# A four-layer graph network on one core: finer buffer waits around two attentions, split first transposes, and a diffusion that runs one tile further ahead

## The chip, the core and the metric

The kernel runs on one core of a Trainium2 chip. The core has five engines that each work through their own queue of instructions in order: TensorE (PE in the profile; its weight loads are listed apart as PEld), VectorE (DVE), ScalarE (ACT), GpSimd (POOL), and SyncE (SP), which here only issues DMA transfers. Engines meet through semaphores. The metric is device time in microseconds (us); three runs of the kernel before took 3431.24 (median), 3437.7 and 3429.77.

## The reference

There are 3327 nodes with 256 features, so 26 row tiles of 128 nodes (3328 rows, one of them padding). Four layers follow one another; each adds its result to x and normalizes:

```python
x = _layernorm(x + _L0_gnn_ref(x, adj, W))        # neighbourhood mean
x = _layernorm(x + _L1_gnn_ref(x, adj, ...))      # graph convolution, then a scan over the nodes
x = _layernorm(x + _L2_gnn_ref(x, adj, ...))      # graph attention
x = _layernorm(x + _L3_gnn_ref(x, adj, ...))      # the layer that changes here
```

Only layer 3 matters here. In its two steps a diffusion and an attention run side by side:

```python
for n in range(2):
    A = _top_p_attention(Xa, W1, W2, W3)   # softmax(q k^T), keep the largest that hold 90%, renormalize
    Xf = R @ Xf                            # R = (adj + I), rows divided by their sums
    Xa = A @ Xa
    Z = Z + Xf @ U1[n].T + Xa @ U2[n].T
h = X + Z                                  # then normalized, scaled and shifted
```

## The kernel before

All data are float32. X holds the input of layer 3 in on-chip memory, tile by tile. F (also named Y) receives the diffused rows, G the attended rows. The program shows each float32 matrix product as two records on PE.

**Who sets the order.** The program is traced in Python and then scheduled at build time: an instruction that is ready earlier may be queued ahead of one traced before it, unless it is pinned. `here(...)`, `in_order(...)` and `keep_in_program_order` pin an instruction behind everything traced before on its engine. In the first attention (`fixed = True`) every PE and DVE instruction made through `tensor` and `vector` is pinned. In the second attention the products of the scores (line 1154), the ScalarE copies and the ScalarE passes of the search are pinned; the products of the diffusion (`aggregated`, line 1296) and of the attention (line 1341), most DVE and POOL work and all DMA issues are not. A queue, once made, runs strictly in order.

**Pools.** Buffers come from pools (`tile_pool`). A pool that opens where an earlier one has closed takes over its memory. Without an option, the first user of such memory waits for the whole earlier pool to be finished with.

**First attention** (lines 1656 to 1770; pools l3p, l3a, and l3w, l3s, which live on through the second). A score row of 128 x 3328 is made in four chunks: PE multiplies, ScalarE copies (lines 1160, 1163). Only one score buffer exists in PSUM, so a chunk waits for the copy of the chunk before it. `search_short` then finds the cut on DVE, with a ScalarE exponential (line 1404) in its middle. Tile 0 is diffused in layer 2 (`spread_first`) and tile 1 by `diffused_first`: four adjacency loads (line 1217), 26 products, a `yield` after every fourth. All others run in pairs of tiles. `diffused_pair` does 13 steps of seven half-size products; `attended_pair` does the same with weights that must first be transposed on PE (`turn`), copied by ScalarE (`wt`, line 1263) and combined on DVE (`mix`). Loop `for i in range(nh - 1)` weaves them: `stage` runs seven diffusion steps; at step 5 `attend_to` flushes the pending search and issues the first three `turn`s, twelve transposes in a row, and two `mix`es. `first` then finishes each tile: two projections, keys and queries of the second attention, stores to DRAM (lines 1569, 1579, 909), and ends with `store_keys` (copies at lines 905 and 907). `unresolved` closes the phase with one small product (line 1627).

**Second attention** (lines 1778 to 1841; pools l3q in PSUM, l3at for the adjacency tiles, l3b for the rest). Loop `for i in range(-2, nt + 1)`; a pass of it is called step i here. Step i makes the scores of tile i+2, goes on with `search_long` of tiles i, i+1 and i+2 (ScalarE lines 1436, 1441, 1456, 1458, 1474, 1487; DVE lines 1503, 1353, 1364, 1366, 1532, 1540), attends tile i-1, and diffuses the tiles named by `more`: before, tile i+1, from step -1 on. `slot` hands out three to five diffusion products between two chunks. A diffusion of one tile (`aggregated`) loads six adjacency pieces through three buffers (line 1294), does 26 products and ends in `xf` (DVE line 1315); `xf` has DL + 3 = 4 buffers. `second` finishes tile i-1 (DVE line 1586, POOL, the output store at line 1608). The scores' buffer is single again, three PSUM buffers serve diffusions and attentions, three the transposes.

Of the kernel before, what the change touches and what calls it, by code (L numbers as in the profile page):

```python
# [9 lines left out]
F32 = mybir.dt.float32  # L10
# [5 lines left out]
PSUM = bass.MemoryType.PSUM  # L16
DRAM = bass.MemoryType.DRAM

P = 128
D = 256  # L20
# [22 lines left out]
DL = 1  # L43
# [7 lines left out]
def gnn_kernel(ctx: ExitStack, tc: tile.TileContext, n: int, a: dict, out: bass.AP):  # L51
    nc = tc.nc
    nt = -(-n // P)
# [814 lines left out]
    with tc.tile_pool(name="l3", bufs=1) as pool, tc.tile_pool(name="l3d", bufs=1, space=DRAM) as dram:  # L868
# [383 lines left out]
        def attended_pair(quads, psum, es, b):  # L1252

            pa = psum.tile([P, 2, 512], F32, name="acc")
            wts, ws = [], []

            def turn(j):
                pt = psum.tile([P, 4, P], F32, name="tp")
                for r, e in enumerate(es):
                    for h in range(2):  # L1260
                        tensor.transpose(pt[:, 2 * r + h, :], e[:, (h * nh + j) * P:(h * nh + j + 1) * P], ident)
                wts.append(quads.tile([P, 4, P], F32, name="wt", bufs=4))
                nc.scalar.copy(wts[-1], pt)  # L1263

            def mix():
                wt = wts.pop(0)
                sw = quads.tile([P, 4, P], F32, name="sw", bufs=3)
                vector.tensor_tensor(sw[:, :2, :], wt[:, ::3, :], wt[:, 2:3, :].to_broadcast([P, 2, P]), op=ALU.add)
                vector.tensor_add(sw[:, 2, :], sw[:, 1, :], wt[:, 0, :])
                vector.tensor_add(sw[:, 3, :], sw[:, 2, :], wt[:, 1, :])  # L1270
                a11, a12, a21, a22, s3, s1, s2, s4 = (x[:, k, :] for x in (wt, sw) for k in range(4))
                ws.append((a11, a12, s1, a22, s2, s3, s4))

            for j in range(3):
                turn(j)
            for j in range(2):
                mix()
            yield None
            for j in range(nh):
                if j + 3 < nh:  # L1280
                    turn(j + 3)
                if wts:
                    mix()
                products(pa, j, ws.pop(0), b)
                yield None
            yield assembled(quads, pa)
# [15 lines left out]
        def diffused(work, atp, psum, p, it, out, each=J3):  # L1302

            rd = rdeg[:, it:it + 1]
            t = work.tile([P, D], F32, name="t")
            nc.gpsimd.tensor_scalar(t, (Y if p else X)[:, it, :], rd, None, op0=ALU.mult)
            if p:
                s = work.tile([P, D], F32, name="s")
                nc.sync.dma_start(s, sd[it])
                nc.gpsimd.tensor_tensor(t, t, s, op=ALU.add)  # L1310
            for acc in aggregated(atp, psum, it, Y if p else X, each):
                if acc is None:
                    yield
            d = work.tile([P, D], F32, name="xf", bufs=DL + 3)
            nc.vector.scalar_tensor_tensor(d, acc, rd, t, op0=ALU.mult, op1=ALU.add)
            out.append(d)

# [318 lines left out]
            while parts:  # L1636
                parts = [x for x in parts if next(x, parts) is not parts]

        with tc.tile_pool(name="l3w", bufs=2) as work, tc.tile_pool(name="l3s", bufs=4) as sm:


            def start(p, t, es, searches, search):
# [7 lines left out]
                                     **({"halves": True} if p and t == nt - 1 else {}))  # L1650
                return scores(work, psum, p, q, es[t])

            with tc.tile_pool(name="l3p", bufs=2, space=PSUM) as psum, tc.tile_pool(name="l3a", bufs=1) as quads:
                fixed = True
                es, searches, xfs, todo, queue = {}, {}, [xf0], [], []
                flat = G.rearrange("p t d -> p (t d)")
# [22 lines left out]
                def stage(spread, steps, groups, ends, counts, then):  # L1679
                    for k in range(steps):  # L1680
                        next(spread, None)
                        then.get(k, int)()
                        if k % 2 == 0:
                            next(groups, None)
                        if k in (2, 3, 4):
                            next(ends[0], None)
                        looks(counts[k])
                    for _ in groups:
                        pass
                    for _ in ends[0]:  # L1690
                        pass

                def attend_to(i):
                    turned[0] = attended_pair(quads, psum, (es[2 * i], es[2 * i + 1]), b)
                    finish()
                    next(turned[0])

                turned = [None]
# [11 lines left out]

                groups = logits(0)
                x = diffused_first(quads, psum, 1, xfs)
                for _ in groups:
                    next(x)
                queue.append(searches[0])
# [8 lines left out]
                counts = 7 * [4]  # L1724
                ends = [iter(())]
                for i in range(nh - 1):
                    stage(spread, 7, logits(2 * i + 2), ends, counts,
                          {0: lambda: end_pair(i - 1) if i else None, 5: lambda: attend_to(i)})
                    counts = [1, 2, 2, 2, 2, 0, 0]
                    queue.append(searches[2 * i + 2])  # L1730
                    values = turned[0]
                    for k in range(7):
                        next(values)
                        looks(k in (1, 2, 4, 5, 6))
                    stage(spread, 6, logits(2 * i + 3), todo[1], [2, 1, 2, 1, 2, 1], {})
                    finish()
                    queue.append(searches[2 * i + 3])
                    for k in range(6):
                        next(values)
                        if k == 0:  # L1740
                            for _ in spread:
                                pass
                        if k == 3:
                            spread = spreading(i + 2)
                        looks(k > 1)
# [29 lines left out]

            with tc.tile_pool(name="l3q", bufs=3, space=PSUM) as psum, tc.tile_pool(name="l3at", bufs=3) as atp, \
                    tc.tile_pool(name="l3b", bufs=2) as lone:
                es, searches, xfs = {}, {}, []  # L1780
                result = iter(())
                for i in range(-2, nt + 1):
                    def search(t):
                        if 0 <= t < nt:
                            next(searches[t])

                    values, logits, spread = iter(()), iter(()), iter(())
                    if 0 < i:
                        values = attended(lone, psum, es[i - 1], G, 3, in_order(nc.scalar.copy))
                    if i + 2 < nt:  # L1790
                        logits = start(1, i + 2, es, searches, search_long)
                    more = range(len(xfs), min(nt, i + DL + 1))
                    spread = (x for j in more for x in diffused(lone, atp, psum, 1, j, xfs, 1))

                    def slot(products, looks, pair=False):


                        if pair:
                            next(logits, None)
                        for _ in range(products * len(more)):  # L1800
                            next(spread, None)
                        if pair:
                            next(logits, None)
                        next(values, None)
                        search(looks)

                    search(i)
                    slot(3, i + 1, True)
                    next(result, None)
                    search(i)  # L1810
                    search(i + 1)
                    search(i)
                    next(logits, None)
                    next(result, None)
                    for _ in range(3 * len(more)):
                        next(spread, None)
                    next(logits, None)
                    search(i + 2)
                    next(values, None)
                    search(i)  # L1820
                    next(result, None)
                    slot(3, i + 1, True)
                    slot(3, i + 1, True)
                    for _ in result:
                        pass
                    both(logits)
                    search(i)
                    slot(5, i + 2)
                    search(i + 1)
                    search(i)  # L1830
                    slot(5, i + 1)
                    slot(4, i + 1)
                    both(spread)
                    search(i)
                    if 0 < i:
                        f = normalizer(sm, kepts[1][:, i - 1:i], tots[1][:, i - 1:i])
                        result = second(lone, psum, i - 1, next(values), f, xfs[i - 1])
                both(result)
                edge[0] = None
                fl = unresolved(sm, psum, 1)  # L1840
# [142 lines left out]
```

## Time and profile before

The profiled execution took 3433.03 us itself; its span on the core is 3431.1 us. Its granted TensorE clock is 0.964 on average.

| engine | busy us | share of span |
|---|---|---|
| PE | 3140.4 | 92% |
| PEld | 2565.8 | 75% |
| DVE | 2686.5 | 78% |
| ACT | 1735.4 | 51% |
| POOL | 1127.6 | 33% |

DMA moved 344.31 MB, a mean of 100 GB/s.

A wait is listed as "engine line <- what released it": total us, number of times, longest. A timeline row gives the start, the length, engine, line, operation, output <- input and count, and in brackets the idle time of the engine before it with what ended it. A row of engine PE with x52 holds 26 products. Line 891 is the helper through which all pinned PE and DVE instructions pass, so there the tile's name tells what it is. Layer 3 begins at about 1699.7 us; in the table of stages that the prediction shows, the stages are the opening of the first attention, its steady part, its end, the opening of the second attention, that attention's next five steps, its steady part, its last step with a diffusion, and the rest.

### The profile page before, as it was taken

The page shows a single profiled execution, that of the slowest core. Times are in us where ns is not written, and L with a number is a line of the kernel's source. Part 1 is how long each engine was busy: PE and PEld are TensorE (multiplying, and loading weights), DVE is VectorE, ACT ScalarE, POOL GpSimd, SP SyncE. Part 2 cuts the span into 40 slices and gives each one's busy share as a digit, 9 for nine tenths or more (in the row PEclk, how much of TensorE's full clock was granted, in tenths as well). Part 3 has the DMA queues.
Part 4 walks back from the last instruction along what each step waited for, and adds up shares of the span by engine and source line. Part 5 has one row for each costly group of instructions (what it writes and reads, how often), then busy time and mean ns, then how long its engine had stood idle before and what let it go on. Part 6 is the DMA issues. An engine that isn't in the chain of part 4 may idle for free. (4 is left out here: it accounts for less than half of the span.)

```text
span 3431.1 us, 50276 instructions
## 1 busy us (share of the span) xinstructions
PE 3140.4 (92%) x18301; PEld 2565.8 (75%) x18301; DVE 2686.5 (78%) x5895; ACT 1735.4 (51%) x2764; POOL 1127.6 (33%) x1332
## 2 busy tenths in 40 slices
PE   8999888898988776999989999999998999999996
PEld 5999657676675554888778888888885677777775
DVE  4655368999999997877578778778755898988886
ACT  1000456767767675111133333333337788888883
POOL 0000245666665654111400000000003566656563
PEclk9999999999999988999999999999998999999998
DMA  6775334334343322444322232232213122222220
GB/s 200 251 253 188 105 101 125 110 108 116 102 115 89 69 57 81 150 137 151 115 76 87 65 88 79 69 89 80 71 50 102 52 68 68 64 66 65 72 64 16
DMA packets 206264, 344.31 MB, mean 100 GB/s; under 512 B 22223, under 2 KB 129167, under 8 KB 205871
## 3 DMA queue, kind: packets, MB, share of 16 engines
q1 hardware_dynamic: 205998, 340.92, 33.2%
q8 instruction: 148, 2.42, 0.3%
q14 instruction: 118, 0.96, 0.1%
HBM read 304.65 MB, written 36.21 MB: 99 GB/s over the span
## 5 line engine op out<-in xcount | busy, mean ns | idle before, releaser
L330 POOL TENSOR_TENSOR h<-du,row 128x2048 f32<-128x2048 f32 (+1 forms) x110 | 465.5, 4232 | 344.9 <-DVE hc L330 248.6
L330 DVE TENSOR_TENSOR_SCAN h<-dA,carry,h 128x512 f32<-128x512 f32 (+1 forms) x384 | 449.0, 1220 | 18.2 <-ACT dA L337 18.1
L337 ACT ACTIVATE dA<-t,A_log 128x512 f32<-128x512 f32 (+1 forms) x448 | 292.5, 658 | 147.1 <-DVE h L330 145.5
L1296 PE MATMUL acc<-F,at 128*128 128x256 f32 x1352 | 354.3, 388 | 1.8 <-DMA at<-in_adjT 1.8
L1341 PE MATMUL acc<-G,wt 128*128 128x256 f32 x1352 | 336.6, 392 | 9.7 <-ACT wt L1139 9.3
L1341 PEld LDWEIGHTS acc<-G,wt 128*128 128x128 f32 x1352 | 250.1, 193 | 72.4 <-ACT wt L1139 42.2
L1079 PE MATMUL acc<-F,at 128*128 128x257 f32 x1352 | 303.4, 381 | 0.7 <-ACT r L1023 0.7
L389 PE MATMUL cb<-F,at 128*128 128x256 f32 x1196 | 295.5, 395 | 8.0 <-ACT hn L409 3.4
L1296 PEld LDWEIGHTS acc<-F,at 128*128 128x128 f32 x1352 | 239.3, 191 | 74.9 <-issue 46.6
L1146 POOL MEMSET e<- 128x1 f32 x52 | 4.9, 99 | 838.5 <-PE tp L891 769.5
L1079 PEld LDWEIGHTS acc<-F,at 128*128 128x128 f32 x1352 | 253.3, 190 | 36.2 <-issue 1.0
L680 PE MATMUL y<-ident,hc 128*128 128x128 f32 x1664 | 236.4, 296 | 46.2 <-DVE hc L330 46.1
L680 PEld LDWEIGHTS y<-ident,hc 128*128 128x128 f32 x1664 | 210.4, 154 | 87.4 <-DVE hc L330 62.6
L389 PEld LDWEIGHTS cb<-F,at 128*128 128x128 f32 x1196 | 229.8, 198 | 58.3 <-issue 19.4
L330 DVE TENSOR_TENSOR hc<-h,row 128x2048 f32<-128x2048 f32 (+2 forms) x114 | 243.2, 2135 | 11.3 <-PE y L680 4.3
L891 PE MATMUL acc<-X,at 128*128 128x128 f32 (+1 forms) x988 | 173.7, 287 | 6.0 <-issue 6.0
L1263 ACT COPY wt<-tp 128x512 f32<-128x512 f32 x156 | 90.8, 589 | 166.6 <-PE tp L891 153.2
L138 PE MATMUL acc<-t,cb 128*128 128x128 f32 (+1 forms) x1014 | 168.4, 275 | 0.0
L891 PEld LDWEIGHTS acc<-X,at 128*128 128x128 f32 x988 | 142.2, 193 | 29.9 <-issue 26.1
L891 PE MATMUL acc<-G,sw 128*128 128x128 f32 x936 | 155.5, 275 | 0.0
L891 DVE MAX8 cand<-e 128x8 f32<-128x128 f32 x676 | 139.8, 277 | 5.0 <-ACT e L1160 3.2
L1160 ACT COPY e<-sc 128x832 f32<-128x832 f32 x78 | 65.9, 845 | 149.2 <-PE sc L891 149.1
(414 smaller groups left out, 7263.0 us busy)
## 6 DMA issues: line engine op xcount, KB each, us to landing
at<-in_adjT SPq DMA_DIRECT2D x54, 832.0 KB, 4.5
at<-in_adjT SPq DMA_DIRECT2D x130, 320.0 KB, 3.0
row<-bc SPq DMA_DIRECT2D x80, 512.0 KB, 5.1
at<-in_adjT SPq DMA_DIRECT2D x52, 640.0 KB, 5.5
at<-in_adjT SPq DMA_DIRECT2D x52, 576.0 KB, 4.1
at<-in_adjT SPq DMA_DIRECT2D x72, 256.0 KB, 3.1
at<-mixed SPq DMA_DIRECT2D x72, 256.0 KB, 3.6
mixed<-cb SPq DMA_DIRECT2D x26, 640.0 KB, 4.2
```

The costliest lines, as they stand in the source:

```text
L138: mm = nc.tensor.matmul(acc, w[:, j, :], x, start=(y == 0 and k % 3 == 0 and k < 6), stop=(y == nh - 1 and k in (2, 6)))
L330: return lambda *x, **k: tc.keep_in_program_order(op(*x, **k))
L337: decays.append(op(*x, **k))
L389: ten.matmul(acc, at[:, j % JC, :], X0[:, j, :], start=(j == 0), stop=(j == nt - 1))
L680: x = ten.matmul(y[:, g * P:(g + 1) * P], h[:, g, i * P:(i + 1) * P], ident, is_transpose=True, start=(first and g == 0), stop=(last and g ...
L891: return lambda *x, **k: tc.keep_in_program_order(op(*x, **k))
L1079: nc.tensor.matmul(acc, at[:, j, :], F[:, j0 + j, :], start=(j0 + j == 0), stop=(j0 + j == nt - 1))
L1146: nc.gpsimd.memset(e[:, n:], NEG)
L1160: copy(halves[:, :, c0:c0 + ws[0]], pl[:, :, :ws[0]])
L1263: nc.scalar.copy(wts[-1], pt)
L1296: nc.tensor.matmul(acc, at[:, j, :], rhs[:, j0 + j, :], start=(j0 + j == 0), stop=(j0 + j == nt - 1))
L1341: tensor.matmul(acc, wt[:, j, :], rhs[:, j0 + j, :], start=(j0 + j == 0), stop=(j0 + j == nt - 1))
```

## The change

Five edits, all in layer 3.

1. The pools l3w, l3s, l3p, l3a, l3q, l3at and l3b get `reuse_waits="tile"`: a buffer waits for the last use of its own memory, not for the end of the pool that had it.
2. `attended_pair` yields after each of its first three `turn`s. `attend_to` issues the first; a new function `go_on` issues the second in the last step of `stage`, and the third after `stage`. The two `mix`es follow the second and the third.
3. `stage` counts the calls in `then` from its end.
4. Two chunks of the first score row are made before the loop that alternates chunks with `diffused_first`.
5. In the second attention `more` names tile i+2, one tile per step, from step -2 on; the last step with a diffusion is 23, not 24. `xf` gets a fifth buffer.

```diff
-            for j in range(3):
-                turn(j)
-            for j in range(2):
-                mix()
+            turn(0)
+            yield None
+            turn(1)
+            mix()
+            yield None
+            turn(2)
+            mix()
             yield None
...
-            d = work.tile([P, D], F32, name="xf", bufs=DL + 3)
+            d = work.tile([P, D], F32, name="xf", bufs=DL + 4)
...
-        with tc.tile_pool(name="l3w", bufs=2) as work, tc.tile_pool(name="l3s", bufs=4) as sm:
+        with tc.tile_pool(name="l3w", bufs=2, reuse_waits="tile") as work, tc.tile_pool(name="l3s", bufs=4, reuse_waits="tile") as sm:
...
-            with tc.tile_pool(name="l3p", bufs=2, space=PSUM) as psum, tc.tile_pool(name="l3a", bufs=1) as quads:
+            with tc.tile_pool(name="l3p", bufs=2, space=PSUM, reuse_waits="tile") as psum, tc.tile_pool(name="l3a", bufs=1, reuse_waits="tile") as quads:
...
-                        then.get(k, int)()
+                        then.get(k - steps, int)()
...
+                def go_on():
+                    next(turned[0])
...
                 x = diffused_first(quads, psum, 1, xfs)
+                next(groups)
+                next(groups)
                 for _ in groups:
                     next(x)
...
-                    stage(spread, 7, logits(2 * i + 2), ends, counts,
-                          {0: lambda: end_pair(i - 1) if i else None, 5: lambda: attend_to(i)})
+                    stage(spread, len(counts), logits(2 * i + 2), ends, counts,
+                          {-7: lambda: end_pair(i - 1) if i else None, -2: lambda: attend_to(i), -1: go_on})
+                    go_on()
...
-            with tc.tile_pool(name="l3q", bufs=3, space=PSUM) as psum, tc.tile_pool(name="l3at", bufs=3) as atp, \
-                    tc.tile_pool(name="l3b", bufs=2) as lone:
+            with tc.tile_pool(name="l3q", bufs=3, space=PSUM, reuse_waits="tile") as psum, tc.tile_pool(name="l3at", bufs=3, reuse_waits="tile") as atp, \
+                    tc.tile_pool(name="l3b", bufs=2, reuse_waits="tile") as lone:
...
-                    more = range(len(xfs), min(nt, i + DL + 1))
+                    more = range(len(xfs), min(nt, i + DL + 2, len(xfs) + 1))
```

## The prediction

> **What bounds the kernel now.** I read the table of stages first, then what PE waited for, then the timelines round each seam of layer 3. In the table each row gives a stretch, its length, the busy time of PE, PEld, DVE, ACT and POOL with their instructions, the granted PE clock, the DMA share and GB/s.
>
> ```profile
> 1699.70:1755.50 55.80, 35.67 (x184) 24.05 (x184) 39.67 (x114) 17.43 (x20) 20.18 (x20) 0.89 0.37 111
> 1755.50:2518.00 762.50, 748.20 (x5805) 666.88 (x5806) 608.92 (x2061) 281.73 (x452) 3.28 (x25) 1.00 0.26 75
> 2518.00:2568.80 50.80, 47.22 (x259) 40.77 (x257) 19.21 (x67) 17.29 (x37) 0.20 (x2) 1.00 0.18 56
> 2568.80:2639.20 70.40, 54.40 (x208) 35.09 (x208) 27.66 (x80) 51.07 (x42) 27.54 (x60) 0.84 0.41 128
> 2639.20:2792.00 152.80, 143.01 (x679) 108.73 (x680) 133.59 (x399) 123.73 (x122) 83.65 (x169) 0.97 0.19 54
> 2792.00:3340.00 548.00, 544.36 (x2617) 405.41 (x2616) 489.85 (x1457) 463.29 (x448) 339.08 (x666) 1.00 0.23 66
> 3340.00:3373.30 33.30, 28.11 (x140) 22.99 (x139) 27.39 (x83) 23.55 (x23) 15.71 (x38) 0.97 0.16 46
> 3373.30:3431.10 57.80, 35.19 (x158) 29.27 (x158) 31.44 (x106) 8.87 (x17) 16.72 (x28) 0.80 0.03 9
> ```
>
> Both long stages are bound by PE: 748.20 of 762.50 us and 544.36 of 548.00 us, at full clock; a step of the second lasts 30.6 us. The seams are not: in the two openings PE stands idle for 20 and 16 us and runs at a lower clock. So the change can win only at seams, and from the 14.3 us missing in the first steady stage, which the list of PE's waits there explains whole:
>
> ```profile
> PE tp L891 <- DVE e L891: 11.7, 11, 1.1
> PE tp L891 <- ACT wt L1263: 2.6, 11, 0.2
> ```
>
> Three rows of the first opening: DVE waits for the end of `diffused_first`, and PE then for the masked score row of tile 1.
>
> ```profile
> 1728.95 0.48 DVE L891 SCALAR_TENSOR_TENSOR F<-acc,rdeg,F 128x256 f32<-128x256 f32 x1 [5.79 <-PE acc L891]
> 1753.69 0.45 PE L891 MATMUL tp<-ident,e 128*128 128x128 f32 x1 [8.89 <-DVE e L891]
> 1755.47 2.27 PE L891 MATMUL tp<-ident,e 128*128 128x128 f32 x9 [1.33 <-DVE e L891]
> ```
>
> The second opening: the first scores wait for the last reader of the old pool; the adjacency is requested late; six products (x12) take 5.14 us, 0.857 us each, where three in the steady part take 1.30, 0.433 each; the first transposes wait 9 us for the search.
>
> ```profile
> 2568.78 1.67 PE L1154 MATMUL sc<-kT,q 64*128 64x416 f32 x4 [1.93 <-ACT q L907]
> 2571.73 1.51 SPq L1294 DMA_DIRECT2D at<-in_adjT  x3
> 2581.31 5.14 PE L1296 MATMUL acc<-F,at 128*128 128x256 f32 x12
> 2639.22 1.97 PE L1327 MATMUL tp<-ident,e 128*128 128x128 f32 x8 [9.00 <-DVE e L1540]
> ```
>
> And step 24, where ScalarE's pass waits behind a copy that waits for PE, and DVE at the end of that chain:
>
> ```profile
> 3350.90 0.58 ACT L1139 COPY wt<-tp 128x512 f32<-128x512 f32 x1 [2.58 <-PE tp L1327]
> 3362.70 0.16 DVE L1490 RECIPROCAL s<-s 128x1 f32<-128x1 f32 x1 [2.79 <-POOL s L1444]
> ```
>
> **What the Trainium skill says.** "TensorE: Matmul & The Clock Gate", section "What's actually happening": PE runs at half clock after some 3.4 us of idling and at full clock after as long of work. The trace agrees: 0.857 against 0.433 us per product. The table at the head of that page calls the ScalarE and VectorE queues strict FIFO; so one late operand holds all behind it, as the 2.58 and 2.79 us show. "DMA: Bandwidth & Descriptors", section "Anatomy of one DMA", puts some 2 us of fixed cost on a transfer, for the software path; here a 320 KB adjacency piece lands 3.0 us after its issue.
>
> **The change, part by part.**
>
> *Two score chunks first* (edit 4). Before, chunk 0 of tile 0 is at 1700.44, chunk 1 only at 1711.13, behind four products that wait for adjacency until 1707.4; chunk 3 at 1717.27. Now chunks 0 to 2 go ahead while that load travels: by 0.97 to 1.46 us of product and 0.85 of copy each, from 1702.88 (first copy, after the table load), they are copied at about 1708; four products at the low clock (3.75) and chunk 3 follow, so the row is copied at 1713.2 against 1719.2. No instruction is added. `spreading(1)` comes two products-of-four earlier, so its three DMAs pass the second adjacency load on SP's queue; that load lands near 1711.5, before PE wants it at 1714. PE then has 22 products (9.5 us), four chunks (3.6) less what is done, and at most 3.2 us behind the exponential: `diffused_first` ends near 1726 instead of 1728.9. On DVE ten looks of the search now precede the wait for it, six before; the four rounds (0.87 each, 3.5 us) fill that wait. From that wait's end to e of tile 1 was 1755.5 - 1728.95 = 26.55; it becomes 23.0. So e is ready at 1749.3: -6.2 us. Bounds: DVE's whole 12.2 us of waiting up to there cannot be beaten; with an end at 1729, 3.5. I take -6.2 and keep -3.5 to -8. Its POOL memset of the padding, at 1718.81 behind 23 row scalings, may cost 1.5, inside these.
>
> *Transposes apart* (edits 2, 3). Same instructions. The 1.06 us wait for e stays: `turn(0)` is still in step 5, and its fourth transpose needs the same DVE result. The 0.24 us wait for the first copy goes, since seven products (1.57 us) stand between: 11 x 0.24 = -2.6. A `cb` subtraction on DVE (0.69) may come ahead of a `mix`; PE has the second and third turn and a chunk (1.9) to cover it; uncovered it costs 0.69 x 12 = 8. Bounds -2.6 to 0, or -14.3 if the e wait vanished too, for which I see no cause.
>
> *Waits by buffer, and the extra diffusion at the seam* (edits 1, 5). Scores can start when line 1627 leaves PE, 2566.9; their copies must still follow `store_keys`, 2568.73. First copy 2568.75 against 2570.53. The adjacency issues move from 2571.7 to before 2550, past the stores of `first` on SP's queue (0.33 to 1.1 us each; SP is idle for most of that time), so products of tile 0 fill the gaps between chunks and keep PE at full clock. A chunk then takes 2.25 us (0.9 + 3 x 0.433) instead of 2.7: the last copy ends 2576.0, not 2579.6. Now the price: 14 products of tile 0 (6.1 us) stand ahead of tile 1's first chunk, pinned behind them. It starts near 2582 (before: 2579.62), so the exponential of line 1441 gains only 0.6; at line 1456, where ScalarE waited 2.84 us for cold products, it is 3.0 ahead, and from there the chain to the transposes is the same 47 us: e at 2636.2, -3.0. Bounds: -6 (no delay behind the products) to +2; beyond that see the rivals.
>
> *Where that work goes.* Before, the opening did three diffusions, one more than its steps name, and steps 1 to 9 issued 420 records of line 1296 instead of 9 x 52 = 468: 24 products, 10.4 us, had been done ahead. With tile i+2 due in step i and three diffusions in the opening, nothing is ahead, and these steps hold 10.4 us more PE work. Their PE waits (0.42, 1.63, 0.37, 2.66, 2.37, 2.32, 0.30) sum to 10.1 us and can take it. I take +2; bounds 0 (hidden) to +10.4. The steady steps keep their content: 30.6 each, 0.
>
> *Step 24 without a diffusion.* Transposes reach ScalarE early; the 2.79 us wait goes and `xf` (0.48) leaves DVE's chain, which then bounds to the end: -3.3 (0 to -4).
>
> Sum: -6.2 - 2.6 - 3.0 + 2.0 - 3.3 = -13.1. The profiled execution took 3433.0 (2 beyond its span, which stays), so 3419.9; the median shown is 1.8 lower: **3418**. Own range 3410 to 3425.
>
> **Rivals.** 0.3% of 3431, 10.3 us, is about what a measurement can tell from no change.
> (a) *The work comes back:* the extra 10.4 us do not fit the waits, since these end with DVE's result at a fixed place in the queue. Sum -4.7 (with +10.4): 3427. For it: PE is the bound in all following steps.
> (b) *The old tail takes it:* with adjacency early, unpinned products slip into PE's gaps (3.6 us from 2518 to 2568) and a fourth diffusion into the 9.0 us before the transposes. 26 x 0.433 = 11.3 more: -24, 3407. Against: before, nothing filled those 9 us.
> (c) *Slower:* adjacency still comes at 2574.8, cold. Three products stand before each pinned chunk, and 26 x 0.857 = 22.3 plus three chunks (5.2) put tile 1's first chunk at 2602, 22.7 late; ScalarE's search stands behind its copy. -6.2 - 2.6 + 22.7 - 3.3 = +10.6: 3442. It decides when that chunk starts after 2602.
> (d) *Pool waits stay in effect* but PE is warm: the chunks wait for 2574.8, +5 in place of -3: -5.1, 3426.
>
> **Chances.** Forecast 0.50, (a) 0.19, (b) 0.14, (c) 0.11, (d) 0.06. Below 3421 lie 0.37 of the forecast's 0.50 and (b): faster 0.51. The rest of the forecast, (a) and (d): same 0.37. (c), with disturbances of the same sign: slower 0.12. Range 3403 to 3435: leaves out (c) and the far edge of (b).
>
> **What the profile will show.** Chunk 3 of tile 0 before 1712.5 and the first masked row near 1749 (else the first step fails); no wait for wt L1263 among PE's waits, 11 to 12 us for e left; adjacency issues before 2560 and PE clock over 0.92 in the opening; its first transposes 66 to 68 us after the first score instead of 70.4; steps of 30.6 after; no 2.79 us DVE wait in step 24. Steps longer than 30.6, or another order on PE in them, would break the forecast: 0.5 us there is 11 us.

## The result: slower by 0.5%

The changed kernel takes 3448.03 us, the kernel before 3430.51 us (medians of six runs each on one chip): the ratio is 1.005, with a 95% interval of 1.0037 to 1.0064, so 12.7 to 22 us more. The forecast was 3418, its range ended at 3435. The profiled span grew from 3431.1 to 3446.6 us.

The table of stages of the changed kernel, with the same columns and cut at the same events as before (first score of layer 3, first attention at work, its last products, first score of the second attention, its first transposes; step 24, the last with a diffusion before, without one now):

```profile
1703.56:1764.00 60.44, 42.60 (x184) 27.95 (x185) 39.60 (x114) 17.43 (x20) 20.20 (x20) 0.78 0.33 103
1764.00:2521.10 757.10, 745.44 (x5805) 666.38 (x5806) 611.88 (x2061) 281.76 (x452) 3.31 (x25) 1.00 0.26 75
2521.10:2569.84 48.74, 47.09 (x256) 40.71 (x255) 18.77 (x64) 16.40 (x34) 1.12 (x3) 1.00 0.17 56
2569.84:2654.79 84.95, 63.87 (x262) 43.99 (x261) 28.30 (x83) 51.97 (x45) 23.36 (x60) 0.88 0.43 129
...
3355.50:3390.00 34.50, 19.08 (x85) 15.70 (x85) 27.70 (x88) 22.01 (x21) 14.47 (x36) 0.84 0.01 5
```

Two stages got shorter: the twelve pairs (757.10 after 762.50) and the end of the first attention (48.74 after 50.80). Three got longer: the first opening (60.44 after 55.80, its clock 0.78 after 0.89), above all the second opening (84.95 after 70.40), and step 24. The steps between them kept their length: from the end of step 0's search to that of step 23 it is 699.6 us, 701.2 before.

**The pairs.** In the list of PE's waits in that stage one row is left; the one for wt L1263 is gone:

```profile
PE tp L891 <- DVE e L891: 13.0, 12, 1.3
```

**The first opening.** The timeline (start, length, engine and line, and in brackets the idle time with what ended it), where before DVE had waited 5.79 us and its row stood at 1728.95:

```profile
1722.69 0.18 POOL L1146 MEMSET e<- 128x1 f32 x4
...
1723.82 3.07 ACT L1407 ACTIVATE e<-e,neg 128x3328 f32<-128x3328 f32 x1 [5.70 <-POOL F L1203]
...
1726.89 0.83 ACT L1160 COPY e<-sc 128x832 f32<-128x832 f32 x1
...
1727.78 1.76 PE L891 MATMUL sc<-kT,q 64*128 64x416 f32 x4 [4.14 <-ACT e L1160]
...
1738.29 0.48 DVE L891 SCALAR_TENSOR_TENSOR F<-acc,rdeg,F 128x256 f32<-128x256 f32 x1 [10.70 <-PE acc L891]
```

The same place before:

```profile
1722.93 3.07 ACT L1404 ACTIVATE e<-e,neg 128x3328 f32<-128x3328 f32 x1 [3.73 <-DVE neg L891]
...
1725.99 0.83 ACT L1160 COPY e<-sc 128x832 f32<-128x832 f32 x1
...
1726.88 0.97 PE L891 MATMUL sc<-kT,q 64*128 64x416 f32 x4 [2.17 <-ACT e L1160]
1727.78 1.13 PE L891 MATMUL acc<-X,at 128*128 128x256 f32 x4
```

Three chunks did go first. Then POOL's memset of the padding, behind its row scalings, holds the end of the first looks and so the exponential: it comes 18.4 us after the first score product, 18.3 before, so it did not move with the chunks. The exponential stands on ScalarE ahead of the copy of tile 1's first chunk, as before, but PE now waits 4.14 us for that copy instead of 2.17. And ten of the 26 products of `diffused_first` are still to come behind that wait, where two were left before, because four products stand between two chunks and two chunks have gone ahead. `diffused_first` ends 34.0 us after the first score product, 28.5 before.

**The second opening**, in the same view:

```profile
2569.84 0.97 PE L1154 MATMUL sc<-kT,q 64*128 64x416 f32 x4
...
2573.07 0.46 SPq L1782 DMA_DIRECT2D G<-gd  x1
...
2574.47 1.58 SPq L1297 DMA_DIRECT2D at<-in_adjT  x3
...
2581.81 2.93 PE L1299 MATMUL acc<-F,at 128*128 128x256 f32 x6 [11.01 <-DMA at<-in_adjT]
...
2584.67 1.76 PE L1154 MATMUL sc<-kT,q 64*128 64x416 f32 x4
...
2599.00 0.97 PE L1154 MATMUL sc<-kT,q 64*128 64x416 f32 x4
...
2654.79 2.39 PE L1330 MATMUL tp<-ident,e 128*128 128x128 f32 x10 [7.93 <-DVE e L1543]
```

The first score starts right behind the last product of the first attention. But the adjacency load is issued 4.6 us after it, and three diffusion products that need it stand ahead of the second chunk: PE waits 11.01 us. Of these, 3.7 us pass until the issue at 2574.47, and 7.3 us from there until the first piece lands at 2581.8. In the steps that follow, such a piece lands after a median of 3.0 us; here the pieces travel right behind the reload of G (1664 KB, issued at 2573.07). Tile 1's first chunk comes 29.16 us after the first score (10.84 before), the transposes 84.95 after (70.44).

**Step 24**, which has no diffusion now (34.2 us from the end of the search in step 23 to that in step 24, 32.7 before):

```profile
3372.82 0.60 ACT L1609 ACTIVATE h<-h,nb,rs 128x256 f32<-128x256 f32 x1 [3.50 <-POOL nb L1608]
...
3375.39 0.16 DVE L1493 RECIPROCAL s<-s 128x1 f32<-128x1 f32 x1 [4.21 <-POOL s L1447]
...
3375.47 0.36 DVE L1367 MAX8 top<-rest 128x8 f32<-128x208 f32 x1
```

The 2.79 us wait did not go: it is 4.21 us, and it now stands in the middle of the ranking of tile 24, with four of its six rounds behind it, where before only the last round was behind it.

The sum over the two profiles: opening (first score to second exponential) +4.55, pairs -5.3, from the last exponential to the first score of the second attention -2.0, second opening +14.5, steps 1 to 23 -1.6, step 24 +1.5: +11.7. The remaining 3.8 us of the span's 15.5 lie ahead of the first score product of layer 3, up to which PE's order is unchanged. In the fourteen profiles of this study that product stands anywhere from 1693.5 to 1704.3 us, so this part is read as variation between runs, which no run here tests; spans of single profiles are therefore not compared below, only stages, and times only as ratios.

### The profile page after: what moved, and what is told of

Same layout as the page of the kernel before. It is cut to its first block, busy times and chain, and to the rows that moved or that the text cites. A ratio compares the mean times of both kernels' runs of the same rounds, so it can differ in the third digit from the quotient of the medians.

```text
span 3446.6 us, 50261 instructions
## 1 busy us (share of the span) xinstructions
PE 3142.4 (91%) x18301; PEld 2569.4 (75%) x18301; DVE 2687.3 (78%) x5895; ACT 1735.6 (50%) x2764; POOL 1129.0 (33%) x1332
## 5 line engine op out<-in xcount | busy, mean ns | idle before, releaser
L330 DVE TENSOR_TENSOR_SCAN h<-dA,carry,h 128x512 f32<-128x512 f32 (+1 forms) x384 | 449.0, 1221 | 18.3 <-ACT dA L337 18.1
L1263 ACT COPY wt<-tp 128x512 f32<-128x512 f32 x156 | 90.7, 591 | 181.4 <-PE tp L891 168.6
L1139 ACT COPY e<-sc 128x832 f32<-128x832 f32 (+2 forms) x130 | 90.0, 713 | 106.9 <-PE sc L1154 105.9
```

The source lines that it names most:

```text
L330: return lambda *x, **k: tc.keep_in_program_order(op(*x, **k))
L1139: return lambda *x, **k: tc.keep_in_program_order(op(*x, **k))
```

## The experiments

Each run was timed against the kernel before on the same chip. "Opening" is the time from the first score product of layer 3 to the second exponential, "pairs" from there to the last exponential of the first attention, "gap" from there to the first score of the second attention, "tile 1" from that score to the first chunk of tile 1, "seam" to the first transposes; step 24 from the start of the pass that writes the masked row e in step 23 to that in step 24. All in us, from the profiles.

| kernel | ratio to before (95%) | opening | pairs | gap | tile 1 | seam | step 24 |
|---|---|---|---|---|---|---|---|
| before | 1 | 45.2 | 777.4 | 45.7 | 10.8 | 70.4 | 32.7 |
| changed | 1.0050 (1.0037 to 1.0064) | 49.8 | 772.1 | 43.7 | 29.2 | 85.0 | 34.2 |
| e1 transposes alone | 0.9991 (0.9983 to 0.9999) | 46.6 | 772.6 | 45.7 | 9.9 | 69.4 | 32.8 |
| e2 two chunks alone | 1.0014 (1.0007 to 1.0021) | 49.6 | 776.8 | 45.7 | 8.2 | 67.1 | 32.7 |
| e3 changed, no edit 5 | 1.0001 (0.9993 to 1.0009) | 51.1 | 771.8 | 43.7 | 10.3 | 68.4 | 32.8 |
| e4 changed, load on POOL | 1.0017 (1.0009 to 1.0026) | 50.7 | 771.8 | 43.7 | 23.5 | 77.5 | 34.2 |
| e5 two chunks, exponential later | 0.9994 (0.9984 to 1.0004) | 41.5 | 778.1 | 45.7 | 10.2 | 70.4 | 32.8 |
| e6 changed, products behind row 0 | 1.0027 (1.0017 to 1.0037) | 50.2 | 771.8 | 43.7 | 25.8 | 83.5 | 34.2 |
| e7 edits 1 to 3, load on POOL | 0.9996 (0.9987 to 1.0005) | 45.9 | 772.1 | 43.7 | 18.1 | 72.6 | 32.8 |
| e8 as e7, with e5 | 0.9984 (0.9977 to 0.9992) | 42.5 | 772.3 | 43.7 | 18.3 | 72.7 | 32.7 |
| e9 edit 5 alone | 1.0031 (1.0019 to 1.0043) | 45.2 | 777.2 | 45.7 | 26.5 | 80.4 | 34.2 |
| e10 pools alone | 1.0007 (0.9997 to 1.0016) | 46.3 | 778.0 | 43.7 | 10.8 | 70.2 | 32.8 |
| e11 changed, step 24 reordered | 1.0041 (1.0026 to 1.0057) | 49.1 | 773.0 | 43.7 | 28.1 | 82.5 | 31.2 |
| e12 edits 1 to 3, e5, e11 | 0.9975 (0.9964 to 0.9986) | 44.1 | 772.2 | 43.7 | 8.9 | 70.2 | 32.3 |

A stage at which two kernels have the same order on the queues still differs between profiles: the seam of before and of e2 is 70.4 and 67.1 us. Differences of 3 us at the seam or 1.5 in the opening are not read as effects. Two stretches are not in the table: steps 1 to 23, which take 698.3 to 702.4 us, and what follows step 24, which takes 61.7 us before and 61.8 in the changed kernel, but 62.9 to 63.4 in e2, e3, e7, e8 and e12; why was not followed.

**e1, the transposes alone.** Edits 2 and 3 of the diff, on the kernel before:

```diff
-            for j in range(3):
-                turn(j)
-            for j in range(2):
-                mix()
-            yield None
+            turn(0)
+            yield None
+            turn(1)
+            mix()
+            yield None
+            turn(2)
+            mix()
+            yield None
```

> Edits 2 and 3 alone on the kernel before. Account of the result read from the two traces: the twelve pairs lose 0.4 us each, so -4.8 us, ratio 0.9986, and the list of PE's waits has no row for wt L1263. Rival: the pairs' gain comes from the tile-wise pools (edit 1) and not from the order of the transposes; then 0 us and the row stays. The prediction's term was -2.6.

The pairs lose 4.8 us, the row for wt L1263 is gone from PE's waits, and the ratio of 0.9991 stands for -3.1 us (-0.3 to -5.8). The gain is the transposes', not the pools': e10 has pairs of 778.0.

**e2, two chunks first, alone.** Edit 4:

```diff
                 x = diffused_first(quads, psum, 1, xfs)
+                next(groups)
+                next(groups)
```

> Edit 4 alone on the kernel before. Account: the two chunks ahead are what costs the first opening its 4.5 us (the exponential of tile 0 stands ahead of tile 1's first copy on ACT, and PE waits behind it), so +4.5 us, ratio 1.0013, second exponential about 50 us after the first score product instead of 45. Rival: the loss comes from edit 1, and edit 4 gives what was predicted, -6.2 us, ratio 0.998.

+4.8 us by the ratio (2.4 to 7.2), and 4.4 in the opening, with the same chain as in the changed kernel:

```profile
1718.13 3.07 ACT L1404 ACTIVATE e<-e,neg 128x3328 f32<-128x3328 f32 x1 [6.69 <-POOL F L1203]
...
1722.08 1.76 PE L891 MATMUL sc<-kT,q 64*128 64x416 f32 x4 [5.14 <-ACT e L1160]
...
1723.77 3.39 PE L891 MATMUL acc<-X,at 128*128 128x256 f32 x8
```

Tile 1's first chunk was multiplied at 1714.05 and copied only at 1721.20, behind the exponential; after the 5.14 us wait four products take 3.39 us, where four took 1.99 ahead of it.

**e5, the same with the exponential later.** On e2, the score copies of tiles 0 and 1 and the first exponential are pinned in the program's order:

```diff
-            copy = in_order(nc.scalar.copy) if p else nc.scalar.copy
+            copy = in_order(nc.scalar.copy) if p or pin else nc.scalar.copy
...
-                return scores(work, psum, p, q, es[t])
+                return scores(work, psum, p, q, es[t], t < 2)
...
-                    nc.scalar.activation(e, e, AF.Exp, bias=neg, accum_out=total)
+                    x = nc.scalar.activation(e, e, AF.Exp, bias=neg, accum_out=total)
+                    if early:
+                        early.pop()
+                        here(x)
```

> Edit 4 alone, with the ScalarE copies of tiles 0 and 1 and the first exponential pinned in the order of the program, which puts the exponential behind tile 1's third copy. Account: what turned edit 4 into a loss is that the exponential, held until POOL's memset of the padding at 1717.0, stands ahead of tile 1's first copy, so PE waits 5.1 us and cools. Then that wait goes and the second exponential comes 41 to 44 us after the first copy (edit 4 alone 47.2, before 42.8): some 4 us less than edit 4 alone, ratio near 1.000. Rival: the loads that were reordered on SP's queue are the cause; then the second exponential stays near 47 and the ratio at 1.0014.

ScalarE in this run, and DVE's wait for `diffused_first`:

```profile
1717.56 0.85 ACT L1139 COPY e<-sc 128x832 f32<-128x832 f32 x1 [1.97 <-PE sc L891]
...
1718.31 3.07 ACT L1406 ACTIVATE e<-e,neg 128x3328 f32<-128x3328 f32 x1
...
1721.43 0.48 DVE L891 SCALAR_TENSOR_TENSOR F<-acc,rdeg,F 128x256 f32<-128x256 f32 x1 [2.18 <-PE acc L891]
```

The copies of tile 1 come first, PE never waits for them, and DVE waits 2.18 us where it waited 10.08 in e2. The second exponential is 39.06 us after the first copy (47.16 in e2, 42.82 before), a little earlier than expected. The order of the exponential and these copies on ScalarE turns edit 4's +4.4 us in the opening into -3.7. The loads had the same order on SP in e2, so the rival falls.

**e3, the changed kernel without edit 5:**

```diff
-            d = work.tile([P, D], F32, name="xf", bufs=DL + 4)
+            d = work.tile([P, D], F32, name="xf", bufs=DL + 3)
...
-                    more = range(len(xfs), min(nt, i + DL + 2, len(xfs) + 1))
+                    more = range(len(xfs), min(nt, i + DL + 1))
```

> The changed kernel with edit 5 undone (tile i+1 again diffused in step i, from step -1; four xf buffers). Account: edit 5 costs 12.5 us at the seam (three products that wait for a late adjacency load stand ahead of tile 0's second chunk) and 1.5 us in step 24. So 14 us less than the changed kernel: ratio to before near 1.001, first score to first transposes at the seam about 70 us instead of 85. Rival: the seam's loss comes from the tile-wise pools and their new queue order; then it stays near 85 us and the ratio at 1.005.

As the account had it: the seam is 68.4 us, step 24 is 32.8, and the ratio falls from 1.005 to 1.0001.

**e9, edit 5 alone**, the same lines the other way round on the kernel before:

```diff
-            d = work.tile([P, D], F32, name="xf", bufs=DL + 3)
+            d = work.tile([P, D], F32, name="xf", bufs=DL + 4)
...
-                    more = range(len(xfs), min(nt, i + DL + 1))
+                    more = range(len(xfs), min(nt, i + DL + 2, len(xfs) + 1))
```

> Edit 5 alone on the kernel before, with the whole-pool waits. Account: the price of edit 5 does not depend on the kind of wait, since the three products that need adjacency stand ahead of tile 0's second chunk either way; seam 82 to 86 us (before 70.4), step 24 34.2 us (before 32.7), ratio 1.0045 to 1.005. Rival: edit 5 is only harmful together with the tile-wise waits, which let the first chunk and the first products start before the stores are done; then the seam stays near 72 us and the ratio at or below 1.001.

Seam 80.4 us, step 24 34.2: edit 5 costs the same kind of time under the old waits. The ratio, 1.0031, is lower than expected (10.6 us; 6.5 to 14.8), and the seam lies under the 82 to 86 us expected.

**e4, the load from another queue.** In `aggregated`, on the changed kernel:

```diff
-                nc.sync.dma_start(at[:, :m, :], a["adjT"][it][:, j0:j0 + m, :])
+                (nc.sync if it else nc.gpsimd).dma_start(at[:, :m, :], a["adjT"][it][:, j0:j0 + m, :])
```

> The changed kernel with tile 0's adjacency loads of the second attention issued from POOL's queue instead of SP's, which takes them out from behind the last tile's stores. Account (the load is late because of SP's order, not because its memory is in use): they are issued before the first score product of the seam, PE's wait of 11.0 us for in_adjT goes, and the seam's 85 us become about 72: 13 us less than the changed kernel, ratio to before near 1.001. Rival A: the memory is what is late, and the issue stays after 2570; no gain. Rival B: the products pinned ahead of the chunks cost the time even when the load is early; then at most 5 us are won, ratio 1.004.

```profile
2552.48 1.39 POOL L1297 DMA_DIRECT2D at<-in_adjT  x2
...
2559.72 0.97 PE L1154 MATMUL sc<-kT,q 64*128 64x416 f32 x4
...
2562.47 0.97 PE L1154 MATMUL sc<-kT,q 64*128 64x416 f32 x4 [0.29 <-ACT e L1139]
...
2576.57 6.71 PE L1299 MATMUL acc<-F,at 128*128 128x256 f32 x22 [4.18 <-DMA at<-in_adjT]
...
2583.21 0.97 PE L1154 MATMUL sc<-kT,q 64*128 64x416 f32 x4
```

The memory was free: issued from POOL, the first two pieces leave 7.2 us ahead of the first score instead of 4.6 behind it. Ahead of the reload of G they land after a median of 3.6 us; the third piece, issued 0.45 us behind that reload, takes 6.5. The 11.01 us wait is gone, the chunks of tile 0 follow each other every 2.4 to 2.75 us, and the last is copied 9.5 us after the first score. So the load was late because of its place on SP, behind the last tile's stores and the reload of G. But the seam falls to 77.5 only: 26 products stand ahead of tile 1's first chunk. The later pieces add to it, since POOL's queue has them behind an addition that waits for a reload of `s` until 2571.55, and PE waits 4.18 us for them. Both the account and rival B were half right.

**e6, all products behind tile 0's row.** On the changed kernel:

```diff
                     more = range(len(xfs), min(nt, i + DL + 2, len(xfs) + 1))
+                    held = len(more) if i > -2 else 0
...
-                        for _ in range(products * len(more)):
+                        for _ in range(products * held):
...
-                    for _ in range(3 * len(more)):
+                    for _ in range(3 * held):
```

> The changed kernel with step -2's diffusion products behind all four chunks of tile 0's row instead of three ahead of each later chunk. Account: at the seam two things cost time, the wait for the load ahead of tile 0's second chunk and the number of products ahead of tile 1's first chunk, which holds ScalarE's search of tile 0. Here the first goes (row of tile 0 copied 11 us after the first product, was 23) but all 26 products stand ahead of tile 1's first chunk, which comes 25 to 30 us after the first product (29.2 in the changed kernel): seam 78 to 84 us, ratio near 1.004. Rival: only the wait ahead of tile 0's second chunk counts; then the seam falls to about 72 us and the ratio to 1.001.

```profile
2574.70 1.75 PE L1154 MATMUL sc<-kT,q 64*128 64x416 f32 x4 [0.95 <-ACT e L1139]
...
2578.82 14.12 PE L1299 MATMUL acc<-F,at 128*128 128x256 f32 x52 [2.37 <-DMA at<-in_adjT]
...
2592.87 0.97 PE L1154 MATMUL sc<-kT,q 64*128 64x416 f32 x4
```

Tile 0's row is copied 10.3 us after the first score, yet the seam is 83.5: the 26 products (x52) take 14.12 us ahead of tile 1's first chunk, whose copy stands on ScalarE ahead of the second exponential of tile 0 and waits 13.22 us. So it is tile 1's first chunk that sets the seam. Over the table, where it comes within 11 us the seam is 67 to 70; at 18 it is 73, at 23 to 29 it is 77 to 85.

**e10, the pools alone:** edit 1 of the diff, on the kernel before. One of its three lines:

```diff
-        with tc.tile_pool(name="l3w", bufs=2) as work, tc.tile_pool(name="l3s", bufs=4) as sm:
+        with tc.tile_pool(name="l3w", bufs=2, reuse_waits="tile") as work, tc.tile_pool(name="l3s", bufs=4, reuse_waits="tile") as sm:
```

> Edit 1 alone on the kernel before. Account: the first scores of the second attention follow 2.0 us sooner behind the first attention's last exponential (43.7 instead of 45.7 us), nothing else: -2 us, ratio 0.9994. What the runs so far leave for it, if the edits add up: 1.0001 without edit 5, less 0.9991 for the transposes and 1.0014 for the chunks, gives 0.9996. Rival: the queue orders it changes in the first opening cost 2 us, as the second exponential at 48.6 to 49.7 us after the first copy, against 47.2 for edit 4 alone, hints; then 0 us.

The gap shrinks by 2.0 us, as read in the changed kernel. The total shows no gain: 1.0007, -1.0 to +5.5 us. The profile has 1.1 us more in the opening and 0.6 in the pairs, each no more than differences between profiles. Where the 2.0 us go is left open.

**e7, edits 1 to 3 with the load from POOL.** Without edits 4 and 5; the first three pieces of tile 0 from POOL:

```diff
-                nc.sync.dma_start(at[:, :m, :], a["adjT"][it][:, j0:j0 + m, :])
+                (nc.gpsimd if it == 0 and j0 < 3 * J3 else nc.sync).dma_start(at[:, :m, :], a["adjT"][it][:, j0:j0 + m, :])
```

> The kernel before with edits 1, 2 and 3, and the first three adjacency loads of the second attention issued from POOL's queue; edits 4 and 5 left out. Account: transposes -3 us, tile-wise pools -2 us (first score right behind the last product of the first attention), and at the seam products that no longer wait for adjacency at a low clock, -2 us: ratio 0.998. Rival: without edit 5 the load is hidden anyway; then -5 us at most, 0.9986 or above.

```profile
2563.40 0.30 POOL L1435 TENSOR_SCALAR neg<-factors,m 128x2 f32<-128x2 f32 x1 [10.60 <-DVE m L1434]
...
2564.07 1.93 POOL L1297 DMA_DIRECT2D at<-in_adjT  x3 [0.37 <-issue]
...
2571.30 2.93 PE L1299 MATMUL acc<-F,at 128*128 128x256 f32 x6 [4.89 <-DMA at<-in_adjT]
```

A miss: 0.9996, and the seam is 72.6, not shorter. The load did not leave early. On POOL it stands behind an instruction of tile 0's search that waits for DVE's first maximum of the scores, so it is issued 4.1 us after the first score product, where e3 has 4.6 from SP. But the order made at build time now has three unpinned products ahead of tile 0's fourth chunk and six ahead of tile 1's first, where e3 has none: PE waits 4.89 us, and tile 1's first chunk comes at 18.1 us instead of about 10. What a load that is early on the chip would give without edit 5 stays open.

**e8, the same with edit 4 as in e5**, that is with these lines and those of e5 added to e7:

```diff
                 x = diffused_first(quads, psum, 1, xfs)
+                next(groups)
+                next(groups)
```

> As the run with edits 1, 2, 3 and the early loads, and edit 4 too, with the exponential behind tile 1's third copy. Account: if edit 4 without its wait gives what the prediction took for it (-6.2 us, at least the lower bound of -3.5), the ratio is 0.9965 to 0.997. Rival: the first opening is bound by DVE's 20 first looks on tile 1's row and by the load of the pair's parts, whatever the order of chunks; then it is the same as without edit 4, about 0.998.

0.9984 (0.9977 to 0.9992): the opening is 42.5 instead of 45.9, the seam again 72.7. The reordered edit 4 does give about what the prediction's lower bound had for it. The ratio falls short of the 0.9965 to 0.997 expected; the seam, with the same late load and the same six products ahead as in e7, is part of that, and the rest was not followed.

**e11, one instruction of step 24 moved.** On the changed kernel:

```diff
-            nc.vector.reciprocal(s, s)
+            with tc.issue_after(ranking[0].ins) if halves else nullcontext():
+                nc.vector.reciprocal(s, s)
...
-                vector.max(top[:, r * 8:(r + 1) * 8], left)
+                ranking[0] = vector.max(top[:, r * 8:(r + 1) * 8], left)
```

> The changed kernel with one DVE instruction moved: the reciprocal of s for the last tile, which waits for POOL in step 24, is put behind the ranking of the tile before it instead of ahead of its last four rounds. Account: step 24 is longer than before because that wait of 4.2 us holds the four rounds; moved behind them, the rounds (0.87 us each, 3.3 us) run in the wait: step 24 30.5 to 31 us instead of 34.2, ratio 1.004. Rival: POOL's queue and the pass of ScalarE behind the output's activation bound the step; then it stays within 1 us of 34.2.

```profile
3361.81 0.38 DVE L1369 MAX8 top<-rest 128x8 f32<-128x208 f32 x1
...
3363.34 0.16 DVE L1496 RECIPROCAL s<-s 128x1 f32<-128x1 f32 x1 [1.16 <-POOL s L1449]
```

All six rounds run ahead of the reciprocal, which then waits 1.16 us instead of 4.21: step 24 is 31.2 us, 3.0 less than in the changed kernel. The ratio, 1.0041 (1.0026 to 1.0057), fits the expected 1.004, but its interval holds 1.005 too; the step's length carries the reading.

**e12, the change without edit 5 and with both orders mended:** edits 1, 2, 3 (edit 1 showed no gain alone), edit 4 in the form of e5, the reciprocal of e11. Against the changed kernel, the lines of e3, e5 and e11:

```diff
-                    more = range(len(xfs), min(nt, i + DL + 2, len(xfs) + 1))
+                    more = range(len(xfs), min(nt, i + DL + 1))
...
+                return scores(work, psum, p, q, es[t], t < 2)
...
+            with tc.issue_after(ranking[0].ins) if halves else nullcontext():
+                nc.vector.reciprocal(s, s)
```

> Edits 1 to 4 with the first exponential behind tile 1's third copy, edit 5 left out, and the reciprocal of s for the last tile behind the ranking. Account, by adding up: transposes -3, pools -1.5, the opening -2 to -4, step 24 -2: about -10 us, ratio 0.997. Rival: the run with the same edits and early loads on POOL (0.9984) already had all of it, and the loads on POOL cost nothing at the seam; then 0.998.

0.9975 (0.9964 to 0.9986), 3421.22 us: faster than the kernel before by 4.8 to 12.4 us, and than the changed one by some 26, by the two ratios. The seam is 70.2 with the load on SP (68.4 in e3), and 72.7 in e8 with it on POOL. The reciprocal gives little here: with a diffusion in step 24 only one round of the ranking stood behind it, and the step is 32.3 us, 0.4 less than before.

## Why the prediction was wrong

It named the right places and, as rival (c) with a chance of 0.11, the mechanism that decided. The step that failed most is the second opening: -3.0 was forecast, and the two stages that make it up measured -2.0 and +14.5. Step by step:

- *Two score chunks first*, taken as -6.2: measured +4.55 in the profile and +4.8 alone (e2). The step that failed is "at most 3.2 us behind the exponential: `diffused_first` ends near 1726". The exponential does take ScalarE for those 3.2 us, but where it stands was not asked: ahead of tile 1's first copy, with ten products left behind it instead of two, and itself held by the memset that was priced at "1.5, inside these". The 4 to 5 us of idling then brought PE to the low clock, which the step did not carry on to the products behind. With the exponential placed later (e5) the same edit gives -3.7 in the opening, near its lower bound of -3.5; the ratio, 0.9994 (0.9984 to 1.0004), lies clear of e2's 1.0014 (1.0007 to 1.0021) but shows no gain over the kernel before.
- *Transposes apart*, -2.6: right, but too small. The waits for wt L1263 went, the waits for e stayed, as said. The pairs lost 5.3 us in the profile (4.8 in e1). The other half is in PE's busy time, 745.44 after 748.20 us with the same 5805 records; which products of a pair became shorter was not followed further. Alone the edit measures -3.1 (-0.3 to -5.8).
- *Waits by buffer, and the extra diffusion at the seam*, -3.0: measured -2.0 for the gap, which is the 1.8 that was predicted for the first copy, and +14.5 for the seam. Three terms failed. First, "the adjacency issues move from 2571.7 to before 2550": the pool's wait was gone and the memory free (e4), but SP runs in order, and the load still stood behind the stores of the last tile: it was issued 48.3 us after the last exponential, 48.7 before. The price for that case was written under (c) but given too little chance. Second, "14 products of tile 0 (6.1 us) stand ahead of tile 1's first chunk": there are 26. Even with the load early (e4) the chunk comes 23.5 us after the first score, where some 15 had been reckoned. Third, "a 320 KB adjacency piece lands 3.0 us after its issue": that is the median of the steps that follow, but the three pieces at this seam took a median of 7.7 us in the profile of before as well, from 2571.73 on. It did not show there, since PE had four more chunks to make until they had landed. So the 2574.8 of rivals (c) and (d) was too early in any case.
- *Where that work goes*, +2.0: the displaced diffusion cost nothing that can be seen, -1.6 for steps 1 to 23, inside what differs between profiles. The premise was off: the opening again did one diffusion more than its steps name, four instead of three, so nothing was displaced. The steady steps stayed at 30.6 us, as forecast.
- *Step 24 without a diffusion*, -3.3: measured +1.5. The transposes did reach ScalarE early, but the search that follows is held by POOL's `nb`, and DVE's order put the wait in the middle of the ranking. With one instruction moved (e11) the step is 31.2: -1.5 to before.
- *Rival (c)*: a late load, three products ahead of each chunk, and ScalarE's search behind the copy of tile 1's first chunk were what decided. That its size came near is in part luck, for two errors offset each other: the load landed at 2581.8, not at 2574.8, but the 26 products took some 14 us, most of them at full clock, not 22.3. Tile 1's first chunk came at 2599.0, ahead of the 2602 that (c) gave as its mark, and 18.3 us later behind the first score than before, where (c) had 22.7; the seam grew by 14.5. Its sum, 3442, still took the gain of the two chunks for granted.

The parts alone (transposes in e1 -3.1, chunks in e2 +4.8, pools in e10 +2.4, edit 5 in e9 +10.6) sum to +14.7 us; the change measured +17.2 (12.7 to 22). So the parts add up within the intervals, and edit 5 is most of it.

## What to carry to other kernels

A wait that is removed only helps if the instruction also moves: on a queue that runs in order, look at what still stands ahead of it, stores and reloads that wait for other engines most of all. That holds for the queue to which it is moved as well (e7). When work is brought ahead, count all of it that lands in front of the next pinned instruction, and ask where the one long instruction of the neighbour engine will stand. And where a planner orders the queues, a late operand in the middle of a row of short instructions can cost more than the work that was taken out.

## What the hardware showed that was not expected

- A wait of 2.17 us left PE's clock about as it was, and waits of 4.14 and 5.14 us brought it down. After the wait of 2.17 us (before, first opening) two products took 1.13 us; after 4.14 and 5.14 us four took 3.78 and 3.39, after no wait 1.99. This agrees with the Trainium skill, "TensorE: Matmul & The Clock Gate", section "What's actually happening", which puts the fall at some 3.4 us of idling. So the wait of 4.14 us cost another 1.8 us on the next four products. The single wait is not all that counts: in the second opening before, chunks that take 0.97 us elsewhere took 1.75 to 1.76 with waits of only 0.95 to 1.01 us between them.
- In all fourteen profiles the adjacency pieces that were issued within 3 us behind the reload of G took 6.5 to 8.0 us to land, and later ones a median of 2.9 to 3.0. No run leaves the reload out, so that it is the cause is argued; the two pieces sent ahead of it in e4 fit.
- A load is hardly dearer to issue from POOL than from SP: three adjacency pieces took 1.68 us to issue (e4), 1.58 on SP (the changed kernel). They landed after a median of 3.6 us, those from SP in the same stretch of e4 after 2.9.
- With PE's order ahead of it unchanged, the first score product of layer 3 moves by up to 10.8 us between profiles (1693.5 to 1704.3): single spans cannot tell kernels 0.3% apart here, stages measured from an event of their own can.
